# LSTM gate products in another order, sums made ahead of product 6, and VectorE work at half steps, in a four-layer graph stack

## The chip, the core and the metric

The kernel runs on one core of a Trainium2 chip. A core has TensorE (PE, matrix products into PSUM), VectorE (DVE), ScalarE (ACT, activations and copies), GpSimd (POOL) and SyncE (SP, which here issues the DMAs). They run side by side and meet at semaphores. The metric is the device time of one execution in microseconds (us), lower is better. Everything is float32.

## What is computed

`x` is 128 batches of 64 tokens with 256 channels. Four layers follow each other, each of the form `x = x + layer(relu(layernorm(x)))`: a graph convolution with batch norm, a graph network with LSTMs over windows of tokens, a causal attention, and a masked four-head attention. The change touches the second layer and the place where it begins. Its core:

```python
def _lstm_last(Wih, Whh, bih, bhh, xs):
    bias = bih + bhh
    def step(carry, x_t):
        h, c = carry
        g = x_t @ Wih.T + h @ Whh.T + bias
        i, f, gg, o = jnp.split(g, 4, axis=-1)
        c = sigmoid(f) * c + sigmoid(i) * tanh(gg)
        h = sigmoid(o) * tanh(c)
        return ((h, c), None)
    ...                                   # zero initial state, last h returned

h = relu(einsum('ts,bsh->bth', adj, x @ Wg0 + bg0))
h = relu(einsum('ts,bsh->bth', adj, h @ Wg1 + bg1))
for p in range(1, MAX_SKIP + 1):          # windows of 1, 2, 3 and 4 tokens
    nw = Tv // p
    wins = h[:, :nw * p, :].reshape(Bv * nw, p, Hd)
    last = _lstm_last(Wih[p-1], Whh[p-1], bih[p-1], bhh[p-1], wins)
    idx = jnp.arange(nw) * p + (p - 1)
    h = h.at[:, idx, :].set(last.reshape(Bv, nw, Hd))
```

Each window length overwrites tokens that the next one reads, and inside a window the tokens follow each other: a chain of recurrences. The batch is cut into 16 chunks of 8 batches. Two chunks make a super-chunk, and the LSTMs run super-chunk by super-chunk (eight of them). In a super-chunk a step multiplies 512 columns in windows of 2, 336 in windows of 3 and 256 in windows of 4.

## The kernel before

**Seven products instead of eight.** A gate's 256 x 256 weight matrix is cut into 2 x 2 blocks of 128, and the columns into two halves. The kernel uses a scheme with 7 products of blocks in place of 8 (numbered 1 to 7), which costs sums on VectorE. A `Unit` is one gate at one token step. Its products go to three PSUM banks: 5 to bank `y`; 2 and 3 to the two halves of bank `z`; 1, 6, 7 and 4 one on top of the other into bank `x`. Each bank's name exists twice. A product has an x part (the token) and an h part (the state); the first token of a window has no h part.

```python
class Unit:
    def __init__(self, q, s):
        self.q, self.s = q, s
        self.banks, self.of = {}, {1: "x", 6: "x", 7: "x", 4: "x", 5: "y", 2: "z", 3: "z"}

    def psum(self, kind):
        return self.banks[self.of[kind]][:, m:n] if kind == 3 else self.banks[self.of[kind]][:, :m]

    def product(self, kind, parts="xh"):
        ...
            nc.tensor.matmul(folded(self.psum(kind)), wsets[p, self.q][:, BLOCKS[kind][i], :],
                             (ox[self.s] if part == "x" else oh)[kind], start=first,
                             stop=(part == "h"), skip_group_check=True)          # L1155

    def copy(self, kind):                                                          # L1161, ScalarE
        nc.scalar.copy(gate(self.q, kind // 5, halves[kind // 5]), self.psum(kind))

    def add(self, dst, a, kind):                                                   # L1164, VectorE
        nc.vector.tensor_add(gate(self.q, *dst), gate(self.q, *a), self.psum(kind))

    def c11(self):
        self.add((0, halves[0]), (0, halves[0]), 2)
    def u4(self):
        self.add((0, halves[1]), (1, halves[1]), 6)
    def c12(self):
        self.add((0, halves[1]), (0, halves[1]), 3)
    def c22(self):
        self.add((1, halves[1]), (1, halves[1]), 7)

    def act(self, part):                                                           # L1084, ScalarE
        if part == 0:
            act(self.q, 0, every, gate(self.q, 0))
        elif part == 1:
            act(self.q, 1, halves[1], gate(self.q, 1, halves[1]))
        else:
            act(self.q, 1, halves[0], self.psum(4))
```

Product 6 adds onto product 1 in bank `x`, so it must come after `copy(1)`; 7 adds onto 6 and must come after the sum that reads 6; 4 must come after `c22`.

**A token step.** Pair A is the gates i and g, pair B the gates f and o. `each(us, f, ...)` applies one function after the other, each to all units of the pair. The order in the program is the order on every engine. At a `yield` other work of the kernel is put in.

```python
A = [Unit(q, 1) for q in (0, 2)]
each(A, pe(5, "x"), pe(3, "x"), pe(2, "x"))
yield
for s in range(1, p):
    last = s == p - 1
    B = [Unit(q, s) for q in (1, 3)]
    if not last:
        ox[s + 1] = operands_x(p, hv, name, s + 1)          # GpSimd
    each(A, pe(5, "h"), do("copy", 5), pe(1), do("copy", 1), pe(3, "h"), pe(6, "x"), pe(6, "h"),
         pe(2, "h"), do("u4"), do("c11"), do("c12"))
    each(B, pe(5), do("copy", 5))
    each(A, do("act", 0), pe(7), do("c22"), do("act", 1))
    each(B[:1], pe(3), pe(2))
    each(A, pe(4), do("act", 2))
    if last:
        load_sets(2)
    nc.gpsimd.tensor_mul(gates[:, 0, :, :n], gates[:, 0, :, :n], gates[:, 2, :, :n])
    each(B[1:], pe(3), pe(2))
    each(B, pe(1), do("copy", 1))
    yield
    each(B, pe(6))
    A = [] if last else [Unit(q, s + 1) for q in (0, 2)]
    each(A, pe(5, "x"))
    ...                                    # cell(): c = c * f, c = c + i * g (VectorE), tanh (ScalarE)
    if last:
        each(B[:1], do("u4"), do("c11"), pe(7))
        each(B[1:], do("u4"), pe(7))
        each(B[:1], do("c22"), do("c12"), do("act", 0))
        each(B[1:], do("c22"), do("c11"), do("c12"), do("act", 0))
        cell(0, every)
    else:
        for u in B:
            each([u], do("u4"), do("c11"), do("c12"), do("act", 0))
        cell(0, every)
        each(B, pe(7), do("c22"))
    each(B, do("act", 1))
    each(A[:1], pe(3, "x"), pe(2, "x"))
    new_state(s, 0, every)
    if not last:
        dh[0]()                            # sums of the new state for the next step, VectorE
    each(A[1:], pe(3, "x"), pe(2, "x"))
    each(B, pe(4))
    ...                                    # act(2), cell and state of the other channel half, dh[1], dh[2]
    yield
```

**What is put in.** While a super-chunk's LSTMs run, the graph convolutions of the next one, the residual sums of the one before and the layernorm of the third layer are put in at numbered yields. Numbers 0 to 3 belong to windows of 1; 4 and 5 open windows of 2, and its only step has 6 in its middle and 7 at its end; windows of 3 have 8 to 13, windows of 4 have 14 to 21. The tables give for each unit of such work its number:

```python
RESIDUAL = (0, 3, 4), (2, 5, 6)
CONV = (3, 4, 4, 5, 6, 7, 8, 9, 10, 10), (3, 4, 4, 11, 12, 13, 14, 15, 16, 17, 18, 20)
BEGUN = (11, 13, 14, 16), (17, 19)
BEGUN_FIRST = (12, 15, 16, 18), (19, 21)
FIRST = (1, 3, 3, 4, 4, 5, 6, 7, 8, 9, 10, 11, 12, 12), (3, 6, 7, 8, 10, 13, 14, 15, 16, 17, 18, 19, 20, 20)
...
START = (0, 1, 0, 0, 0, 1, 0, 1, 1, 0, 0, 1, 1, 0, 1)        # convolutions of chunks 0 and 1, ahead of the LSTMs
```

A convolution's units are, in order: batch norm scale and transposes (VectorE) and a DMA out and back; a sum; layernorm statistics; two halves of the layernorm apply (ScalarE); aggregation (TensorE); copies; product v; its bound (VectorE); product u; its bias (VectorE); a second aggregation; two activations. `FIRST` is the table of the first super-chunk.

Of the kernel before, what the change touches and what calls it, by code (L numbers as in the profile page):

```python
# [19 lines left out]
def kernel(  # L20
# [23 lines left out]
    B, T, D = x.shape  # L44
# [544 lines left out]
    with tc.manual_schedule(engines={mybir.EngineType.PE, mybir.EngineType.DVE,  # L589
# [27 lines left out]
        for c in range(2, NCH - 1):  # L617
            a, z = sevens[c], sevens.get(c - 1)
# [146 lines left out]
    with tc.manual_schedule(engines={mybir.EngineType.PE, mybir.EngineType.DVE,  # L765
# [3 lines left out]
        for c in range(2, NCH - 1):  # L769
            a, b, z = sevens[c], sevens.get(c + 1), sevens.get(c - 1)  # L770
# [121 lines left out]
    hTs = {}  # L892
# [157 lines left out]
    def lstm(p, hv, name, follows, x1, ending):  # L1050
# [3 lines left out]
        n = nb * nw  # L1054
# [85 lines left out]
        class Unit:  # L1140
# [25 lines left out]
            def c11(self):  # L1166
                self.add((0, halves[0]), (0, halves[0]), 2)

            def u4(self):
                self.add((0, halves[1]), (1, halves[1]), 6)  # L1170

            def c12(self):
                self.add((0, halves[1]), (0, halves[1]), 3)

            def c22(self):
                self.add((1, halves[1]), (1, halves[1]), 7)
# [9 lines left out]
        def each(us, *fs):  # L1186
            for f in fs:
                for u in us:
                    f(u)

        def pe(kind, parts="xh"):
            return lambda u: u.product(kind, parts)

        def do(f, *a):
            return lambda u: getattr(u, f)(*a)
# [4 lines left out]
        for s in range(1, p):  # L1200
            last = s == p - 1
            B = [Unit(q, s) for q in (1, 3)]
            if not last:
                ox[s + 1] = operands_x(p, hv, name, s + 1)
            each(A, pe(5, "h"), do("copy", 5), pe(1), do("copy", 1), pe(3, "h"), pe(6, "x"), pe(6, "h"),
                 pe(2, "h"), do("u4"), do("c11"), do("c12"))
            each(B, pe(5), do("copy", 5))
            each(A, do("act", 0), pe(7), do("c22"), do("act", 1))
            each(B[:1], pe(3), pe(2))
            each(A, pe(4), do("act", 2))  # L1210
            if last:
                load_sets(2)
            nc.gpsimd.tensor_mul(gates[:, 0, :, :n], gates[:, 0, :, :n], gates[:, 2, :, :n])  # L1213
            each(B[1:], pe(3), pe(2))
            each(B, pe(1), do("copy", 1))
            yield
            each(B, pe(6))
            A = [] if last else [Unit(q, s + 1) for q in (0, 2)]
            each(A, pe(5, "x"))

            def cell(c, part):
                nc.vector.tensor_mul(cells[:, c, part], cells[:, c, part], gate(1, c, part))
                nc.vector.tensor_add(cells[:, c, part], cells[:, c, part], gate(0, c, part))  # L1223
                nc.scalar.activation(gate(2, c, part), cells[:, c, part], AF.Tanh)  # L1224

            if last:

                each(B[:1], do("u4"), do("c11"), pe(7))
                each(B[1:], do("u4"), pe(7))
                each(B[:1], do("c22"), do("c12"), do("act", 0))  # L1230
                each(B[1:], do("c22"), do("c11"), do("c12"), do("act", 0))
                cell(0, every)
            else:
                for u in B:
                    each([u], do("u4"), do("c11"), do("c12"), do("act", 0))
                cell(0, every)
                each(B, pe(7), do("c22"))
            each(B, do("act", 1))
            each(A[:1], pe(3, "x"), pe(2, "x"))
            new_state(s, 0, every)  # L1240
            if not last:
                dh[0]()
            each(A[1:], pe(3, "x"), pe(2, "x"))
            each(B, pe(4))
            B[0].act(2)
            cell(1, halves[1])
            B[1].act(2)
            cell(1, halves[0])
            new_state(s, 1, halves[1])
            if not last:  # L1250
                dh[1]()
            new_state(s, 1, halves[0], nc.gpsimd if follows and last else nc.vector)
            if last:
                load_sets(2)
                ending()
            else:
                dh[2]()
            yield
# [212 lines left out]

    RESIDUAL = (0, 3, 4), (2, 5, 6)
    CONV = (3, 4, 4, 5, 6, 7, 8, 9, 10, 10), (3, 4, 4, 11, 12, 13, 14, 15, 16, 17, 18, 20)
    BEGUN = (11, 13, 14, 16), (17, 19)
    BEGUN_FIRST = (12, 15, 16, 18), (19, 21)
    FIRST = (1, 3, 3, 4, 4, 5, 6, 7, 8, 9, 10, 11, 12, 12), (3, 6, 7, 8, 10, 13, 14, 15, 16, 17, 18, 19, 20, 20)
    AHEAD = (4, 5, 7, 12, 14, 15), (6, 7)
    LATE = 5, 6, 8, 9  # L1480
    IDLE = {5: 4, 7: 18, 9: 10, 13: 14, 15: 8}
    FINAL = (4, 5, 10, 12, 12, 14), (6, 7, 11, 14, 14, 16)
    START = (0, 1, 0, 0, 0, 1, 0, 1, 1, 0, 0, 1, 1, 0, 1)

    tc.no_sync_barrier()
    with tc.manual_schedule(engines={mybir.EngineType.PE, mybir.EngineType.DVE, mybir.EngineType.Pool,
# [21 lines left out]
    with tc.manual_schedule(engines={mybir.EngineType.PE, mybir.EngineType.DVE, mybir.EngineType.Pool,  # L1508
                                     mybir.EngineType.Activation, mybir.EngineType.SP}):
        last = NCH // SUP - 1  # L1510
        for sc in range(last + 1):
# [23 lines left out]
            if sc + 1 < last:  # L1535
                for i in range(SUP):
                    units((BEGUN if sc else BEGUN_FIRST)[i], convs[(sc + 2) * SUP + i])
            for n, _ in enumerate(lstms(sc, hTs[sc])):
                for u in todo.pop(n, ()):
                    next(u)  # L1540
                if sc == last and n in IDLE:
                    keep_busy(IDLE[n], f"l{n}")
                if sc == last and n == 8:

                    new_hT(sc + 1)
                    for c in range(SUP):
                        load2(c, hTs[sc + 1][:, c, :].rearrange("p (q n) -> p q n", q=Q))
# [530 lines left out]
```

## Time and profile before

The median of 3 runs is 1892.07 us (1891.79 to 1892.09).

| engine | busy us | share of the span | instructions |
|---|---|---|---|
| TensorE, matmul | 1863.0 | 99% | 15077 |
| TensorE, weight load | 1479.3 | 78% | 15077 |
| VectorE | 1236.6 | 65% | 3150 |
| ScalarE | 1016.6 | 54% | 2284 |
| GpSimd | 551.4 | 29% | 704 |

The profile is one execution, with a span of 1890.8 us. The LSTM products of line 1155 run from 306 to 1516 us. In the timeline each line names the start, the duration, the engine, the source line, output and input, the shape and the count; in brackets stands how long the engine had been idle and what ended it. In the groups the columns are the count, the busy time, the mean of one in ns, the idle time before them and what ended it. A product's end is modelled, so a busy TensorE may still start late; the spacing of starts shows it.

### The profile page before, as it was taken

How to read it: one execution, taken by the hardware profiler on the slowest of the kernel's cores; microseconds unless marked ns; L12 is line 12 of the kernel's file. 1: busy time of each engine (PE TensorE's matmuls, PEld its weight loads, DVE VectorE, ACT ScalarE, POOL GpSimd, SP SyncE). 2: the span in 40 equal slices, each digit the busy share in tenths (PEclk: the TensorE clock that was granted, in tenths of full speed). 3: DMA queues.
4: the chain of work that ended last, by engine and by line, in shares of the span. 5: the costliest groups of instructions: out<-in, count | busy, mean ns of one | idle time of the engine just before them, and what ended most of it. 6: DMA issues, size and time to landing. Idle time of an engine off the chain costs nothing.

```text
span 1890.8 us, 39088 instructions
## 1 busy us (share of the span) xinstructions
PE 1863.0 (99%) x15077; PEld 1479.3 (78%) x15077; DVE 1236.6 (65%) x3150; ACT 1016.6 (54%) x2284; POOL 551.4 (29%) x704
## 2 busy tenths in 40 slices
PE   8999989999999999999999999999999999999998
PEld 6877856886897798699589689878969967777776
DVE  6768845567476666667667666665565567676776
ACT  5766544456456446555655645655565544444453
POOL 5856622122222212212322321222122114332232
PEclk9999999999999999999999999999999999999999
DMA  3224643135333433332433343343144254444433
GB/s 114 73 66 150 234 175 105 49 116 184 106 129 139 151 129 129 110 124 114 151 118 139 141 151 129 129 135 117 52 135 154 71 157 135 143 148 142 139 113 113
DMA packets 111273, 241.45 MB, mean 128 GB/s; under 512 B 11504, under 2 KB 74864, under 8 KB 111088
## 3 DMA queue, kind: packets, MB, share of 16 engines
q1 hardware_dynamic: 110192, 237.09, 37.4%
q8 instruction: 119, 1.95, 0.4%
q0 software_dynamic: 320, 1.05, 0.2%
q10 hardware_dynamic: 576, 0.82, 0.1%
q14 instruction: 66, 0.54, 0.1%
HBM read 170.50 MB, written 68.42 MB: 126 GB/s over the span
## 4 chain that ended last, share of the span: by engine, by line
PE 90%; DVE 5%; ACT 2%; issue 1%; POOL 1%; DMA 1%; SPq 0%; DVEq 0%; ACTq 0%
PE x L1155 23%; PE z L1155 11%; PE g L1126 9%; PE y L1155 6%; PE v L1568 6%; PE x L1329 4%; PE y L1329 3%; PE u L929 3%; PE p_q L1575 3%; PE v L915 3%; PE X L1764 3%; PE X L423 2%; PE X L499 2%; PE Y L1764 1%; PE Y L423 1%
## 5 line engine op out<-in xcount | busy, mean ns | idle before, releaser
L1164 DVE TENSOR_TENSOR gates<-gates,x 128x128 f32<-128x128 f32 (+2 forms) x384 | 118.5, 321 | 326.3 <-PE x L1155 319.1
L1155 PE MATMUL x<-xd,wset 128*128 128x128 f32 (+2 forms) x1152 | 256.8, 311 | 0.7 <-DVE gates L1164 0.2
L1155 PE MATMUL x<-hd,wset 128*128 128x128 f32 (+2 forms) x1152 | 246.7, 303 | 0.0
L1213 POOL TENSOR_TENSOR gates<-gates 128x512 f32<-128x512 f32 (+2 forms) x48 | 75.0, 1562 | 551.8 <-ACT gates L1084 551.8
L1084 ACT ACTIVATE gates<-gates,bias 128x256 f32<-128x256 f32 (+4 forms) x384 | 170.3, 490 | 56.2 <-DVE gates L1164 52.7
L1155 PEld LDWEIGHTS x<-xd,wset 128*128 128x128 f32 x1152 | 180.8, 190 | 19.0 <-DVE gates L1164 6.1
L1155 PEld LDWEIGHTS x<-hd,wset 128*128 128x128 f32 x1152 | 185.1, 191 | 5.0
L1126 PE MATMUL g<-hT,wset 128*128 128x256 f32 (+2 forms) x576 | 183.9, 474 | 1.1 <-DVE hT L1095 1.1
L1126 PEld LDWEIGHTS g<-hT,wset 128*128 128x128 f32 x576 | 108.6, 190 | 69.8 <-issue 38.5
L1161 ACT COPY gates<-y 128x128 f32<-128x128 f32 (+2 forms) x192 | 54.3, 294 | 202.3 <-PE y L1155 201.8
L1155 PE MATMUL z<-hs,wset 128*128 128x128 f32 (+2 forms) x768 | 154.0, 303 | 0.0
L1155 PE MATMUL z<-hT,wset 128*128 128x128 f32 (+2 forms) x768 | 148.4, 306 | 0.0
L1155 PEld LDWEIGHTS z<-hs,wset 128*128 128x128 f32 x768 | 119.8, 191 | 3.3
L1155 PEld LDWEIGHTS z<-hT,wset 128*128 128x128 f32 x768 | 117.9, 192 | 4.4 <-ACT gates L1113 0.5
L1161 ACT COPY gates<-x 128x128 f32<-128x128 f32 (+2 forms) x192 | 56.6, 296 | 93.5 <-PE x L1155 92.8
L1164 DVE TENSOR_TENSOR gates<-gates,z 128x128 f32<-128x128 f32 (+2 forms) x384 | 104.5, 316 | 0.1
L1084 ACT ACTIVATE gates<-x,bias 128x128 f32<-128x128 f32 (+2 forms) x192 | 74.8, 390 | 49.3 <-PE x L1155 46.5
L1113 ACT ACTIVATE gates<-g,bias 128x512 f32<-128x512 f32 (+2 forms) x144 | 74.6, 560 | 30.7 <-PE g L1126 30.2
L1155 PE MATMUL x<-hT,wset 128*128 128x128 f32 (+2 forms) x384 | 85.7, 305 | 0.4 <-ACT gates L1084 0.2
L1155 PE MATMUL x<-hs,wset 128*128 128x128 f32 (+2 forms) x384 | 84.9, 303 | 0.0
L1224 ACT ACTIVATE gates<-cell 128x256 f32<-128x256 f32 (+2 forms) x144 | 55.3, 384 | 51.9 <-DVE cell L1223 50.3
L1155 PE MATMUL y<-xd,wset 128*128 128x128 f32 (+2 forms) x384 | 77.4, 304 | 3.9 <-ACT gates L1113 3.3
(326 smaller groups left out, 4144.6 us busy)
## 6 DMA issues: line engine op xcount, KB each, us to landing
wset<-wfar SPq DMA_DIRECT2D x96, 960.0 KB, 6.5
hT<-far_h SPq DMA_DIRECT2D x124, 128.0 KB, 3.1
far_h<-hm SPq DMA_DIRECT2D x16, 512.0 KB, 2.8
far_n<-xs SPq DMA_DIRECT2D x16, 512.0 KB, 3.5
xs<-far_n SPq DMA_DIRECT2D x64, 128.0 KB, 3.7
far_x<-xs SPq DMA_DIRECT2D x16, 512.0 KB, 3.0
x<-far_x SPq DMA_DIRECT2D x64, 128.0 KB, 3.2
xt<-in_x_dram SPq DMA_DIRECT2D x15, 512.0 KB, 4.1
```

Source lines behind the costliest of these rows:

```text
L423: nc.tensor.matmul(self.banks[tag][:, i * CH // 2 : (i + 1) * CH // 2], w, self.at[kind], start=first and not i, stop=True, skip_group_che ...
L915: nc.tensor.matmul(banks[m], wg0_sb[:, k, m * P : (m + 1) * P], agg[:, k, :], start=(k == 0), stop=(k == KD - 1))
L1084: nc.scalar.activation(gate(q, c, part), src, AF.Tanh if q == 2 else AF.Sigmoid, bias=bs[:, q * KD + c : q * KD + c + 1])
L1113: nc.scalar.activation(columns_of(gate(q, c)), natural(banks[q, c][:, :n].rearrange("p (w b) -> p w b", b=nb)), AF.Tanh if q == 2 else AF. ...
L1126: nc.tensor.matmul(banks[q, c][:, :n].rearrange("p (w b) -> p w b", b=nb), wsets[p, q][:, 2 * k + c, :], hv[:, k, : (nw - 1) * p + 1 : p, ...
L1155: nc.tensor.matmul(folded(self.psum(kind)), wsets[p, self.q][:, BLOCKS[kind][i], :], (ox[self.s] if part == "x" else oh)[kind], start=firs ...
L1161: nc.scalar.copy(gate(self.q, kind // 5, halves[kind // 5]), self.psum(kind))
L1164: nc.vector.tensor_add(gate(self.q, *dst), gate(self.q, *a), self.psum(kind))
L1213: nc.gpsimd.tensor_mul(gates[:, 0, :, :n], gates[:, 0, :, :n], gates[:, 2, :, :n])
L1329: nc.tensor.matmul(folded(ps(g, kind)), wih1[:, g, KINDS1[kind], :], right[kind], start=kind in (2, 5, 1), stop=True, skip_group_check=True)
L1568: nc.tensor.matmul(ps[:, i, :], hT[:, k, j, :], w[:, k, first : first + D], start=(k == 0), stop=(k == KD - 1))
L1764: nc.tensor.matmul(st[c, tag][:, i * CH // 2 : (i + 1) * CH // 2].rearrange("p (a n) -> p a n", n=P), w, st[c, "o7"][kind], start=first an ...
```

## The change

The sums of a gate are taken in another order. With `v5` the sum of blocks 5 and 3 is made first, and `u5` adds product 6 to it, where before `u4` added 6 to 5 and `c12` added 3 after it. So the sums with 2, 3 and 5 can be made before product 6 is there, and after it one sum is left instead of three. The products 3 and 2, which share bank `z`, both come before the first sum that reads the bank. Between the products 1 and 6 of pair B the second unit's product 3 now stands (and its product 2, except in the last step of a window, where product 2 stands between 6 and 7).

A new `yield "a"` in the first half of a step gets half numbers (5.5, 9.5, 11.5 and so on); VectorE work that stood in the second half of a step moves there. In the first super-chunk, the first unit of the convolution of chunk 2 moves into the start phase, and the chunk's other units one place ahead.

```diff
-            def u4(self):
-                self.add((0, halves[1]), (1, halves[1]), 6)
-
-            def c12(self):
-                self.add((0, halves[1]), (0, halves[1]), 3)
+            def v5(self):
+                self.add((0, halves[1]), (1, halves[1]), 3)
+
+            def u5(self):
+                self.add((0, halves[1]), (0, halves[1]), 6)
...
-            each(A, pe(5, "h"), do("copy", 5), pe(1), do("copy", 1), pe(3, "h"), pe(6, "x"), pe(6, "h"),
-                 pe(2, "h"), do("u4"), do("c11"), do("c12"))
+            each(A, pe(5, "h"), do("copy", 5), pe(1), do("copy", 1), pe(3, "h"), pe(2, "h"), do("v5"),
+                 do("c11"), pe(6), do("u5"))
             each(B, pe(5), do("copy", 5))
             each(A, do("act", 0), pe(7), do("c22"), do("act", 1))
-            each(B[:1], pe(3), pe(2))
+            yield "a"
+            each(B[:1], pe(3))
             each(A, pe(4), do("act", 2))
             if last:
                 load_sets(2)
             nc.gpsimd.tensor_mul(gates[:, 0, :, :n], gates[:, 0, :, :n], gates[:, 2, :, :n])
-            each(B[1:], pe(3), pe(2))
+            each(B[:1], pe(2), do("v5"))
             each(B, pe(1), do("copy", 1))
+            each(B[:1], do("c11"))
+            each(B[1:], pe(3))
+            if not last:
+                each(B[1:], pe(2), do("v5"), do("c11"))
             yield
             each(B, pe(6))
+            if last:
+                each(B[1:], pe(2))
             A = [] if last else [Unit(q, s + 1) for q in (0, 2)]
             each(A, pe(5, "x"))
...
+            each(B[:1], do("u5"))
             if last:
-
-                each(B[:1], do("u4"), do("c11"), pe(7))
-                each(B[1:], do("u4"), pe(7))
-                each(B[:1], do("c22"), do("c12"), do("act", 0))
-                each(B[1:], do("c22"), do("c11"), do("c12"), do("act", 0))
+                each(B[1:], do("v5"), do("c11"))
+            each(B[1:], do("u5"))
+            each(B, do("act", 0), pe(7))
+            if last:
+                each(B, do("c22"))
                 cell(0, every)
             else:
-                for u in B:
-                    each([u], do("u4"), do("c11"), do("c12"), do("act", 0))
                 cell(0, every)
-                each(B, pe(7), do("c22"))
+                each(B, do("c22"))
...
-    RESIDUAL = (0, 3, 4), (2, 5, 6)
-    CONV = (3, 4, 4, 5, 6, 7, 8, 9, 10, 10), (3, 4, 4, 11, 12, 13, 14, 15, 16, 17, 18, 20)
+    RESIDUAL = (0, 3, 4), (2, 5, 5.5)
+    CONV = (3, 4, 4, 5, 5.5, 7, 8, 9, 10, 10), (3, 4, 4, 11, 11.5, 13, 14, 15, 15.5, 17, 18, 20)
     BEGUN = (11, 13, 14, 16), (17, 19)
-    BEGUN_FIRST = (12, 15, 16, 18), (19, 21)
-    FIRST = (1, 3, 3, 4, 4, 5, 6, 7, 8, 9, 10, 11, 12, 12), (3, 6, 7, 8, 10, 13, 14, 15, 16, 17, 18, 19, 20, 20)
+    BEGUN_FIRST = (11.5, 15, 17, 18), (19, 21)
+    FIRST = (1, 2, 3, 4, 5, 5.5, 7, 8, 9, 9.5, 11, 12, 12), (3, 5.5, 7, 8, 10, 13, 14, 15, 15.5, 17, 17.5, 19, 20, 20)
...
-    START = (0, 1, 0, 0, 0, 1, 0, 1, 1, 0, 0, 1, 1, 0, 1)
+    START = (0, 1, 0, 0, 0, 1, 0, 1, 1, 0, 0, 1, 1, 0, 1, 2)
...
-            for n, _ in enumerate(lstms(sc, hTs[sc])):
+            n = -1
+            for mark in lstms(sc, hTs[sc]):
+                n = n + 0.5 if mark else int(n) + 1
```

## The prediction

> **What bounds the kernel now.** I read the page's busy shares first, then its chain, then the costliest groups.
>
> ```profile
> PE 1863.0 (99%) x15077; PEld 1479.3 (78%) x15077; DVE 1236.6 (65%) x3150; ACT 1016.6 (54%) x2284; POOL 551.4 (29%) x704
> ...
> PE 90%; DVE 5%; ACT 2%; issue 1%; POOL 1%; DMA 1%; SPq 0%; DVEq 0%; ACTq 0%
> ...
> L1164 DVE TENSOR_TENSOR gates<-gates,x 128x128 f32<-128x128 f32 (+2 forms) x384 | 118.5, 321 | 326.3 <-PE x L1155 319.1
> ```
>
> TensorE is the bound and no product is removed, so only TensorE's own gaps can be won. VectorE idles 319.1 us waiting for the products of L1155, which by itself costs nothing. "99%" hides gaps, because each record's modelled end reaches past the next start. So I went to the timeline and measured starts. A product (x part and h part) is four records; back to back they start every 0.112 us at 128 columns (window 4), 0.143 at 168 (window 3), 0.216 at 256 (window 2). An ordinary step of window 4:
>
> ```profile
> 872.28 0.39 PE L1155 MATMUL x<-hT,wset 128*128 128x128 f32 x2
> ...
> 872.48 0.27 ACT L1161 COPY gates<-x 128x128 f32<-128x128 f32 x1 [0.97 <-PE x L1155]
> 872.50 0.39 PE L1155 MATMUL x<-hs,wset 128*128 128x128 f32 x2
> ...
> 872.80 0.49 PE L1155 MATMUL x<-xd,wset 128*128 128x128 f32 x2
> ...
> 875.75 0.48 DVE L1164 TENSOR_TENSOR gates<-gates,x 128x128 f32<-128x128 f32 x2
> ...
> 876.08 0.49 PE L1155 MATMUL x<-xd,wset 128*128 128x128 f32 x2
> ```
>
> At 872.80 product 6 of pair B starts 0.30 after 872.50, not 0.22, because it waits for the copy that ends at 872.75; the pair then takes 0.49, not 0.39: the record after a late one is another 0.10 late. So a wait costs its lateness plus 0.10. Product 4 at 876.08 does the same after the sum c22. The last step of a window has a third such place, product 7 at 901.68:
>
> ```profile
> 901.34 0.29 DVE L1164 TENSOR_TENSOR gates<-gates,x 128x128 f32<-128x128 f32 x1 [3.97 <-PE x L1155]
> ...
> 901.68 0.49 PE L1155 MATMUL x<-xd,wset 128*128 128x128 f32 x2
> ...
> 902.77 0.49 PE L1155 MATMUL x<-xd,wset 128*128 128x128 f32 x2
> ```
>
> Summing spacing beyond the regular pace over all 5376 records of L1155 gives 34.0 us, about 3.5 in each of the eight super-chunks and 8.0 in the first. That is 1.8% of 1892, and the ceiling of the main part of the change. By place, over the run: ordinary steps, product 6 of B 3.5 and product 4 of B 4.0; last steps of windows 3 and 4, product 6 of B 2.1, 7 of B 3.7, 4 of B 2.4; product 7 of pair A in step 2 of window 4, 1.6; start of its step 3, 3.3; product 5 right after an aggregation, 4.8 (not touched); the rest is small, but for the first super-chunk:
>
> ```profile
> 306.19 2.39 ACT L1113 ACTIVATE gates<-g,bias 128x512 f32<-128x512 f32 x4
> ...
> 307.00 1.18 PE L1155 MATMUL y<-xd,wset 128*128 128x256 f32 x4 [2.51 <-ACT gates L1113]
> ...
> 308.06 3.59 PE L1155 MATMUL z<-hT,wset 128*128 128x256 f32 x8
> ```
>
> ```profile
> 308.30:311.70 3.40, 3.40 (x12) 2.13 (x15) 2.69 (x5) 2.58 (x5) 0.00 (x0) 0.50 0.99 230
> ```
>
> ScalarE stood behind four layernorm applies (304.21 to 306.28) of convolution chunk 2, TensorE idled 2.5 us, and then ran at a granted clock of 0.50 (the third number from the end) for 3.4 us: eight z records each 0.21 late, 1.7 us. Together about 4.5 us.
>
> **What the Trainium skill says.** "Perfetto Trace Analysis", Identifying the Most-Contended Engine: matmul busy time is no measure of nearness to the roof. The trace agrees: 99% busy, with 34 us of late starts in one line. "TensorE: Matmul & The Clock Gate", Part 2, LDWEIGHTS: TensorE pulls the next weight load ahead of running matmuls. The 0.10 us after each late record fits a load that could not be pulled ahead; that reading is mine. The same page, Part 1: an idle window of about 3.4 us drops the clock to half. Here it was 0.50 for 3.4 us after only 2.5 us of idling; the measured state decides. "PSUM — Partial Sum Buffer", bank collisions: accesses of two engines must be guarded by bank, not by address. That explains the order "both products of a bank, then its reads". Whether the program really waits by bank no view of this kernel shows, as it never reads one half of bank z between the products 3 and 2. I take it as likely and use it below.
>
> **The change, part by part.** Counts of matmuls, copies, sums and activations do not change; only orders do. Latencies from the timeline at 128 columns: start of a product's last record to the VectorE sum 0.38, to a ScalarE copy 0.31; sum 0.29, or 0.20 apart in a row; copy 0.27; end to the waiting product 0.05.
>
> *Ordinary steps (window 3 step 1, window 4 steps 1 and 2).* Products 3 and 2 of B's second unit now lie between products 1 and 6, so copy 1 has 0.89 us more: it ends long before product 6. After product 6 VectorE has two sums left instead of six. With product 6 of B at 0: u5 of the two units at 0.72 and 1.16, sigmoid 1.04 to 1.55, cell product 1.59, cell sum 2.12, c22 2.46 to 2.74, so product 4 may start at 2.80, where TensorE arrives at 3.13. Both waits vanish: -3.5 - 4.0 = -7.5 us.
>
> *Last steps (one per window).* Product 2 of B's second unit fills the place between 6 and 7. That removes the waits at 6, 7 (first unit) and 4, 8.2 us, plus 0.3 in window 2. But product 7 of the second unit must wait for u5 of that unit, which VectorE takes only after v5 and c11, and these need product 2. Window 4, product 6 at 0: the last record of product 2 starts at 1.23, v5 at 1.61, c11 1.81, u5 2.01 to 2.29, product 7 at 2.34 against 1.79: late by 0.55 + 0.10 = 0.65. By the same count in windows 3 and 2 also about 0.65. Three per super-chunk: 3 x 0.65 x 8 = +15.6. If v5 is not held by product 2, one sum less: 0.47, 0.41 and 0.29, +9.3. Net +7 or +1.
>
> *Pair A, start of a step.* u5 now comes fifth of six sums, not first, and must be done before product 7 of A. With VectorE free there is 0.6 us of slack. Where other VectorE work comes first there is less:
>
> ```profile
> 882.30 0.45 DVE L1164 TENSOR_TENSOR gates<-gates,x 128x128 f32<-128x128 f32 x2
> ...
> 882.60 0.30 PEld L1155 LDWEIGHTS x<-xd,wset 128*128 128x128 f32 x2 [0.25 <-DVE gates L1164]
> ```
>
> Here (window 4 step 2) a scaling and two transposes end at 882.3. Four sums more ahead would make it 0.8 worse in the five super-chunks where it occurs, +4. Against this stands that the whole recurrence (c22, cell, tanh, state) ends about 1.4 us earlier by my count above, and so this work starts earlier. I take -1. The start of step 3 (3.3 us) waits for the same recurrence: I take -1.5.
>
> *Other VectorE work moved to the half steps.* Taken out of the second half it no longer stands behind v5 and c11 in VectorE's queue. In the old kernel it already ran at that time (its sums L935 began at 869.56, right after c22 of A): no gain of its own, a condition of the first part.
>
> *First super-chunk.* The first unit of convolution chunk 2 moves into the start phase, where VectorE is idle between 274.1 and 279.6 and the unit needs 2.3 (286.54 to 288.88). Its chain then runs one place earlier throughout, the applies come before ScalarE is needed, and the wait with its half clock goes: -4.5. The late first product 5 at 291.38 (0.46), held by sums behind the same unit, goes too: -0.5.
>
> Sum with the bank rule: -7.5 + 7 - 1 - 1.5 - 5 = -8. Without it: -14. I weigh them about 2 to 1: -10, so 1882.
>
> **Rivals.** (1) The new wait at product 7 eats the gain: the change only moves waits in the last steps. For it: VectorE's queue order; against it: one product earlier everything else. With VectorE slower than counted (L1223 and L1222 take 0.43 and 0.55 beside GpSimd at 877.3 and 877.7) and no gain at the clock: about 1890. (2) Pair A becomes the bound: 0.5 to 1 us more at product 7 of A in several steps, 8 to 15 us: 1890 to 1897. For it: the 882.6 wait; against it: in the other steps the slack is 0.5 us or more. (3) All waits named go and no new one counts: -7.5 - 8 - 1.6 - 3.3 - 5 = -25, 1867. Against it: u5 of the second unit can't precede its product 2.
>
> **Range and chances.** The three rivals span 1867 to 1897. Each needs several places to err the same way, so 1873 to 1891 should hold 8 in 10. To be faster by 2% it would have to save 38 us, more than all 34 us of late starts; slower by 2% would need about 0.8 us of new waiting in each of the 48 token steps.
>
> **What will show it.** A super-chunk lasts 155.57 us now (start of window 2 to the next, in the middle of the run): I expect 0.4 to 1.2 less. No 0.49 pairs at products 6 and 4 of B in ordinary steps; a new one at the second product 7 of each last step, waiting on L1164 for 0.3 to 0.6; no clock of 0.50 near 308. I am wrong if pair A's product 7 waits in most steps, if VectorE's queue delays the state at a step's end, or if the first super-chunk finds another wait.

## The result: 0.4% slower, and where the time went

The changed kernel takes 1899.49 us (median of 4 runs, 1899.12 to 1900.02), beside 1891.93 us for the kernel before. The ratio is 1.0042 with a 95% interval of 1.0024 to 1.0059: 7.6 us more, where 10 us less was predicted. It lies above the predicted range of 1873 to 1891.

From the page of the changed kernel: the busy times, the chain that ended last, and three groups (the products of `x`, and the sums that read `z` and `x`; the last columns are the idle time before them and what ended most of it).

```profile
PE 1857.2 (98%) x15077; PEld 1478.1 (78%) x15077; DVE 1253.9 (66%) x3150; ACT 1020.8 (54%) x2284; POOL 548.0 (29%) x704
...
PE 87%; DVE 7%; ACT 2%; issue 1%; POOL 1%; DMA 1%; SPq 0%; DVEq 0%; ACTq 0%
...
L1155 PE MATMUL x<-xd,wset 128*128 128x128 f32 (+2 forms) x1152 | 260.8, 308 | 17.1 <-DVE gates L1164 16.6
L1164 DVE TENSOR_TENSOR gates<-gates,z 128x128 f32<-128x128 f32 (+2 forms) x384 | 108.1, 319 | 188.6 <-PE z L1155 141.3
...
L1164 DVE TENSOR_TENSOR gates<-gates,x 128x128 f32<-128x128 f32 (+2 forms) x384 | 117.0, 321 | 116.4 <-PE x L1155 115.4
```

Counts of instructions are the same. TensorE is still the bound, but the chain's VectorE share went from 5% to 7%, and the products of bank `x` now show 16.6 us of idling behind the sums of L1164; before there were 0.2 us. VectorE's own idling before the sums that read `x` fell from 326.3 to 116.4 us, but most of it only moved to the sums that read `z` and now come first: 188.6 us, where the kernel before had 0.1. TensorE's waits, added up (waiting line, what ended it, us in all, times, the longest):

```profile
PE x L1155 <- DVE gates L1164: 16.6, 40, 1.3
PE g L1126 <- DMA wset<-wfar: 3.1, 1, 3.1
```

The second line is one wait for weights, in the first super-chunk, which the kernel before did not have. This view sees only a part, since a record that starts late often counts as no idling. Measured as in the prediction, as spacing of the starts beyond the regular pace, the late starts of L1155 rose from 34.0 to 40.5 us; an ordinary super-chunk has 5.0 where it had 3.5, and lasts 157.05 us where it lasted 155.56. By place, in us over the whole run:

| place | before | after |
|---|---|---|
| product 6 of B (ordinary and last steps) | 5.6 | 0 |
| first product 7 of B, last steps | 3.7 | 0 |
| second product 7 of B, last steps | 0.3 | 14.2 |
| product 4 of B, ordinary steps | 4.0 | 3.0 |
| product 4 of B, last steps | 2.4 | 2.45 |
| product 7 of A (window 4 steps 2 and 3, window 3 step 2) | 1.6 | 9.1 |
| product 7 of B in the last super-chunk, ordinary steps | 0 | 2.6 |
| start of step 3 of window 4 (products 1 and 5 of A) | 3.3 | 1.15 |
| first super-chunk: weights (L1126), with the half clock after them | 0 | 4.9 |

An ordinary step of the changed kernel, window 4 step 1, in the timeline:

```profile
719.39 0.39 PE L1155 MATMUL x<-xd,wset 128*128 128x128 f32 x2
...
719.59 0.49 DVE L1164 TENSOR_TENSOR gates<-gates,z 128x128 f32<-128x128 f32 x2 [0.76 <-PE z L1155]
...
719.99 0.16 DVE L194 SCALAR_TENSOR_TENSOR nmr_b<-mv_b,rstd_b 128x4 f32<-128x4 f32 x1
...
720.06 0.70 DVE L1164 TENSOR_TENSOR gates<-gates,x 128x128 f32<-128x128 f32 x2
720.18 1.09 ACT L196 ACTIVATE cv<-xs,nmr_b,rstd_b 128x256 f32<-128x256 f32 x2 [1.22 <-DVE nmr_b L194]
...
721.18 0.89 ACT L1084 ACTIVATE gates<-gates,bias 128x256 f32<-128x256 f32 x2
...
722.57 0.48 DVE L1164 TENSOR_TENSOR gates<-gates,x 128x128 f32<-128x128 f32 x2
...
722.91 0.49 PE L1155 MATMUL x<-xd,wset 128*128 128x128 f32 x2 [0.24 <-DVE gates L1164]
```

Product 6 of B at 719.39 starts on time and its pair takes 0.39, so the copy no longer holds it: that half of the plan worked. Then a small operation that belongs to the work put in, the shift `nmr` of a layernorm (0.16 us), stands in VectorE's queue behind v5 and c11 and just ahead of the two sums with product 6. ScalarE has idled 1.22 us for it; then it makes two layernorm applies (1.09 us from 720.18), and the sigmoids of pair B stand in its queue behind them (721.18). So they begin 1.79 us after product 6, where the prediction counted 1.04, and the kernel before had 1.54. Product 4 at 722.91 is late and takes 0.49, as before. Pair A of the next step:

```profile
729.12 0.84 DVE L1164 TENSOR_TENSOR gates<-gates,z 128x128 f32<-128x128 f32 x4
...
729.89 0.47 DVE L1164 TENSOR_TENSOR gates<-gates,x 128x128 f32<-128x128 f32 x2
...
730.22 0.49 PE L1155 MATMUL x<-xd,wset 128*128 128x128 f32 x2 [0.84 <-DVE gates L1164]
```

The two sums that product 7 of A needs (reading `x`, at 729.89) stand behind four sums that read `z`, which take 0.84 us, and TensorE idles 0.84 us for them. Beyond the regular pace, with the record after it, that is 1.11 us each time, in five super-chunks; the kernel before lost 0.32 here. And the last step of a window:

```profile
748.92 0.49 DVE L1164 TENSOR_TENSOR gates<-gates,z 128x128 f32<-128x128 f32 x2 [0.60 <-PE z L1155]
...
749.32 0.48 DVE L1164 TENSOR_TENSOR gates<-gates,x 128x128 f32<-128x128 f32 x2
...
749.65 0.49 PE L1155 MATMUL x<-xd,wset 128*128 128x128 f32 x2 [0.33 <-DVE gates L1164]
...
750.75 0.49 PE L1155 MATMUL x<-xd,wset 128*128 128x128 f32 x2
```

VectorE had been idle 0.60 us for product 2 of the second unit; then v5, c11 and u5 follow in a row and product 7 starts late at 749.65. The first super-chunk, first where the old wait stood and then where a new one came:

```profile
303.93 1.03 PE L1155 MATMUL y<-xd,wset 128*128 128x256 f32 x4
304.80 1.89 PE L1155 MATMUL z<-hT,wset 128*128 128x256 f32 x8
...
377.22 2.14 SPq L887 DMA_DIRECT2D wset<-wfar  x4
...
379.47 1.99 PE L1126 MATMUL g<-hT,wset 128*128 128x256 f32 x8 [0.16 <-DVE hT L1095]
...
384.56 3.79 PE L1126 MATMUL g<-hT,wset 128*128 128x256 f32 x11 [3.09 <-DMA wset<-wfar]
```

The eight `z` records take 1.89 us at the full clock, not 3.59. But the weights of window 4, issued at 377.22, hold TensorE up at 384.56. In SyncE's queue they now stand behind a store (372.17), four loads (from 374.90) and one more load (376.69) of a later convolution, whose first unit the change moved from number 12 to 11.5 (`BEGUN_FIRST`); in the kernel before the first two of these four weight issues came at 376.43, ahead of that store at 377.41. After 3.1 us of idling the clock fell again (windows view: the window and its length, busy time and count of PE, PEld, DVE, ACT and POOL, clock, DMA share, GB/s):

```profile
386.00:389.40 3.40, 3.40 (x10) 2.74 (x9) 0.51 (x2) 2.02 (x5) 0.00 (x0) 0.52 0.99 413
```

So the first super-chunk took 162.88 us (159.69 before), after it had begun its windows of 2 earlier by 3.07 us.

### The profile page after: what moved, and what is told of

Same layout as the page of the kernel before. It is cut to its first block, busy times and chain, and to the rows that moved or that the text cites. A ratio compares the mean times of both kernels' runs of the same rounds, so it can differ in the third digit from the quotient of the medians.

```text
span 1897.5 us, 39094 instructions
## 1 busy us (share of the span) xinstructions
PE 1857.2 (98%) x15077; PEld 1478.1 (78%) x15077; DVE 1253.9 (66%) x3150; ACT 1020.8 (54%) x2284; POOL 548.0 (29%) x704
## 4 chain that ended last, share of the span: by engine, by line
PE 87%; DVE 7%; ACT 2%; issue 1%; POOL 1%; DMA 1%; SPq 0%; DVEq 0%; ACTq 0%
PE x L1155 21%; PE z L1155 11%; PE g L1126 9%; PE y L1155 5%; PE v L1576 5%; PE x L1335 4%; PE y L1335 3%; PE v L915 3%; PE u L929 3%; PE p_q L1583 3%; PE X L1772 3%; PE X L423 2%; PE X L499 2%; DVE gates L1164 2%; PE Y L1772 1%
## 5 line engine op out<-in xcount | busy, mean ns | idle before, releaser
L1155 PE MATMUL x<-xd,wset 128*128 128x128 f32 (+2 forms) x1152 | 260.8, 308 | 17.1 <-DVE gates L1164 16.6
L1155 PE MATMUL x<-hd,wset 128*128 128x128 f32 (+2 forms) x1152 | 254.7, 303 | 0.0
L1164 DVE TENSOR_TENSOR gates<-gates,z 128x128 f32<-128x128 f32 (+2 forms) x384 | 108.1, 319 | 188.6 <-PE z L1155 141.3
L1155 PEld LDWEIGHTS x<-xd,wset 128*128 128x128 f32 x1152 | 186.3, 191 | 34.3 <-DVE gates L1164 27.8
L1164 DVE TENSOR_TENSOR gates<-gates,x 128x128 f32<-128x128 f32 (+2 forms) x384 | 117.0, 321 | 116.4 <-PE x L1155 115.4
L1155 PEld LDWEIGHTS x<-hd,wset 128*128 128x128 f32 x1152 | 187.8, 191 | 5.0
L1126 PE MATMUL g<-hT,wset 128*128 128x256 f32 (+2 forms) x576 | 185.6, 477 | 3.3 <-DMA wset<-wfar 3.1
L1126 PEld LDWEIGHTS g<-hT,wset 128*128 128x128 f32 x576 | 109.8, 192 | 72.2 <-issue 42.1
L1155 PE MATMUL z<-hT,wset 128*128 128x128 f32 (+2 forms) x768 | 146.7, 303 | 0.0
L1155 PE MATMUL z<-hs,wset 128*128 128x128 f32 (+2 forms) x768 | 146.5, 303 | 0.2 <-DVE hs L1093 0.2
L1155 PEld LDWEIGHTS z<-hT,wset 128*128 128x128 f32 x768 | 117.2, 191 | 3.7
L1155 PEld LDWEIGHTS z<-hs,wset 128*128 128x128 f32 x768 | 117.2, 191 | 3.6 <-DVE hs L1093 0.3
L1155 PE MATMUL x<-hT,wset 128*128 128x128 f32 (+2 forms) x384 | 85.7, 305 | 0.2 <-ACT gates L1084 0.2
L1155 PE MATMUL x<-hs,wset 128*128 128x128 f32 (+2 forms) x384 | 84.9, 303 | 0.0
L1155 PE MATMUL y<-hd,wset 128*128 128x128 f32 (+2 forms) x384 | 79.4, 309 | 0.0
```

Source lines behind the costliest of these rows:

```text
L1126: nc.tensor.matmul(banks[q, c][:, :n].rearrange("p (w b) -> p w b", b=nb), wsets[p, q][:, 2 * k + c, :], hv[:, k, : (nw - 1) * p + 1 : p, ...
```

## The experiments

The theory after the comparison was that five separate waits, each caused by an order in a queue, make up the loss and hide a gain: pair A's sums, product 7 of the last steps, the shift ahead of product 6's sums, the DMA issues of the first super-chunk, and units of the last super-chunk that stayed at whole numbers. The general rival was that the waits only shift the recurrence: take one away and the next holds the same chain, so that little comes back. Each is undone alone, then all together; some runs try a second way or ask about one part. All ratios are to the kernel before, so the changed kernel stands at 1.0042. Its interval reaches from 1.0024 to 1.0059, so for the savings of 3 to 5 us below the waits that go in the traces weigh more than the times.

**Pair A's sums in the old order.** Only the order of pair A's sums goes back; its products keep the new order (2 ahead of 6), and everything else stays as changed.

```diff
-            each(A, ..., pe(3, "h"), pe(2, "h"), do("v5"), do("c11"), pe(6), do("u5"))
+            each(A, ..., pe(3, "h"), pe(2, "h"), pe(6), do("u4"), do("c11"), do("c12"))
```

> The changed kernel (1899.5 us) with one part undone: pair A takes its sums in the old order (block 5 plus product 6 first, then 2, then 3). Theory: in pair A, u5 stands fifth behind four sums, and where other VectorE work comes first this makes product 7 of A late; the trace of the changed kernel shows 5.6 us at step 2 and 2.8 us at step 3 of windows of 4, 0.7 at step 2 of windows of 3. Then the waits fall to about 1.6 us in all and the time to about 1892. Rival: the recurrence itself ends late and VectorE is busy anyway, the order within pair A does not matter: 1898 to 1900.

Measured: 1891.43 us, ratio 0.9999 (0.9991 to 1.0008), 0.43% or 8.1 us below the changed kernel. TensorE's idling behind the sums of L1164 falls from 16.6 to 11.3 us. Product 7 of A in window 4 step 2 is back at 1.6 us, the ones in step 3 and in window 3 are gone, and the late starts of L1155 fall from 40.5 to 33.1. So no new wait took its place. The rest of the saving (8.1 against 7.4) lies behind the LSTMs, in a stretch that is 1.0 us shorter in this run; the part on the sum below comes back to it. This one line of the program undoes the whole loss.

**The second unit of the last step summed in the old way.** u4 (5 + 6) directly after product 6, then product 7, and the sums with 2 and 3 behind it.

```diff
             if last:
-                each(B[1:], do("v5"), do("c11"))
-            each(B[1:], do("u5"))
-            each(B, do("act", 0), pe(7))
+                each(B[1:], do("u4"))
+                each(B[:1], do("act", 0))
+                each(B, pe(7))
+                each(B[1:], do("c11"), do("c12"), do("act", 0))
```

(`c22` follows, and ordinary steps keep the changed order.)

> The changed kernel with another order of VectorE in the last step of a window, second unit of pair B: block 5 plus product 6 first, then product 7 may go, and the sums with 2 and 3 after it. TensorE's order is as in the changed kernel. Theory: the second product 7 waits for a sum that stands behind two sums that need product 2; the trace shows 14.2 us of this (0.59 in each of 24 last steps). It goes, against up to 2.5 us that may come back at product 4: about 1886 to 1888. Rival: the wait only moves to the sums after it and to the state at the end of the step, so that less than 4 us are won: 1896 or more.

Measured: 1884.89 us, ratio 0.9962 (0.9949 to 0.9975), 0.80% or some 15 us below the changed kernel. Its last step:

```profile
744.84 0.29 DVE L1164 TENSOR_TENSOR gates<-gates,x 128x128 f32<-128x128 f32 x1 [0.75 <-PE x L1155]
...
745.35 0.29 DVE L1164 TENSOR_TENSOR gates<-gates,x 128x128 f32<-128x128 f32 x1 [0.23 <-PE x L1155]
...
745.53 0.39 PE L1155 MATMUL x<-xd,wset 128*128 128x128 f32 x2
...
745.73 0.48 DVE L1164 TENSOR_TENSOR gates<-gates,z 128x128 f32<-128x128 f32 x2
...
745.98 0.39 PE L1155 MATMUL x<-xd,wset 128*128 128x128 f32 x2
```

Each sum with product 6 now waits only for its product (the `x` sums at 744.84 and 745.35), the sums that read `z` come behind, and both products 7 run in pairs of 0.39. The late starts fall by 14.4 us, to 26.1, and a super-chunk takes 155.29 us. Product 4 keeps its wait of 2.57 us, and it doesn't grow by what product 7 no longer waits.

**Product 2 of the last step as early as in ordinary steps.** Another way to the same end: product 2 of the second unit, v5 and c11 ahead of product 6.

```diff
             each(B[1:], pe(3))
-            if not last:
-                each(B[1:], pe(2), do("v5"), do("c11"))
+            each(B[1:], pe(2), do("v5"), do("c11"))
             yield
             each(B, pe(6))
-            if last:
-                each(B[1:], pe(2))
...
-            if last:
-                each(B[1:], do("v5"), do("c11"))
```

> The changed kernel with TensorE's order in the last step of a window as in ordinary steps: product 2 of pair B's second unit before product 6, with v5 and c11 there. Theory: the wait at the second product 7 comes only from product 2 standing between 6 and 7; it goes (14.2 us), and in its place the first product 7 has nothing between it and product 6, and waits for u5 by 0.27 in windows of 4 and 0.17 in windows of 3 (3.5 us in all): about 1889. Rival: VectorE is the bound of the last step, and the wait stays wherever product 2 stands: 1896 or more.

Measured: 1889.34 us, ratio 0.9986 (0.9978 to 0.9993), 0.56% or 10.6 us less. The wait at the second product 7 is gone. At the first product 7 one of 2.45 us in all appears, since nothing stands any more between the products 6 and 7 of the pair; I had expected 3.5. The run before it, with the old sums there, is 4.5 us better; it keeps product 2 as a filler and lets no sum that is due wait for it. These waits explain about 2.5 of the 4.5.

**Is it the bank or the data?** v5 reads the half of bank `z` that product 3 wrote, not that of product 2. In the changed kernel product 2 stands ahead of v5 in the program. Here only that order is turned; v5 stays as it is.

```diff
             if last:
-                each(B[1:], pe(2))
+                each(B[1:], do("v5"), pe(2))
...
             if last:
-                each(B[1:], do("v5"), do("c11"))
+                each(B[1:], do("c11"))
```

> The changed kernel, but in the last step v5 of pair B's second unit stands in the program ahead of product 2 of that unit, which shares its bank. Theory: a read of a bank waits for every product that stands ahead of it in the program and writes this bank, also to the other half; v5 then no longer waits for product 2, one sum fewer lies between product 2 and the second product 7, and the wait there falls from 0.59 to about 0.4, 0.4 and 0.3 in windows of 4, 3 and 2: 4 to 5 us less, about 1895. Rival: waits go by the half that is read, v5 was already early: 1899 to 1900.

Measured: 1894.02 us, ratio 1.0014 (1.0006 to 1.0023), 0.28% or 5.3 us less. The wait at the second product 7 falls from 14.2 to 9.7 us: 0.47, 0.43 and 0.32 each in windows of 4, 3 and 2. Its last step:

```profile
746.34 0.29 DVE L1164 TENSOR_TENSOR gates<-gates,z 128x128 f32<-128x128 f32 x1 [0.67 <-PE z L1155]
...
746.54 0.48 DVE L1164 TENSOR_TENSOR gates<-gates,x 128x128 f32<-128x128 f32 x2
...
746.88 0.49 PE L1155 MATMUL x<-xd,wset 128*128 128x128 f32 x2 [0.20 <-DVE gates L1164]
```

Only one sum (c11) now waits for product 2, where two did. The prediction's count without the bank rule was 9.3 us for this place; so in the changed kernel the read of one half did wait for the product that the program put ahead of it in the other half. The rest of the wait is plain order: c11, which nobody needs soon, stands in the queue ahead of u5, and it needs product 2.

**The shift of the layernorm on GpSimd.** To take the small operation out of VectorE's queue.

```diff
-        nc.vector.scalar_tensor_tensor(nmr, mv[:, :, 0], -1.0, rstd, op0=OP.mult, op1=OP.mult)
+        nc.gpsimd.tensor_tensor(nmr, mv[:, :, 0], rstd, OP.mult)      # right behind the statistics
+        nc.gpsimd.tensor_scalar(nmr, nmr, -1.0, None, op0=OP.mult)
```

> The changed kernel, but the small layernorm shift (128x4) in front of the applies of convolutions and of the third layer is made by GpSimd right after the statistics, not by VectorE at the place of the applies. Theory: at number 16 the shift stands in VectorE's queue behind v5 and c11, the applies of ScalarE start late, the sigmoids of pair B behind them too, and so product 4 of B (2.5 us at step 1 of windows of 4); with the shift made earlier these go, and the recurrence ends earlier, so that product 7 of A in step 2 wins 1 to 2 us as well: about 1895. Rival: ScalarE is late for another reason: no change, 1899 to 1900.

Measured: 1898.67 us, ratio 1.0033 (1.0021 to 1.0045), 0.09% less, inside the uncertainty: a miss in the total. Product 4 of B in window 4 step 1 lost its wait (2.51 to 0), so that cause was right. But about 3 us of new waits came at the start of the windows of 2, at products 5 and 3: 0.78 in each of four super-chunks. One of them:

```profile
777.55 2.08 ACT L201 ACTIVATE cv<-xs,nmr_b,rstd_b 128x256 f32<-128x256 f32 x4 [5.38 <-POOL nmr_b L194]
```

The applies wait for GpSimd's two operations, which take 0.76 and 0.55 us there (from 776.13), beside a sum on VectorE; behind the applies stand the activations that product 5 waits for. In two other super-chunks, where that VectorE sum begins about when they end, the two operations take 0.20 and 0.24 us, and product 5 is on time. So the new cost is a later shift again, in front of ScalarE. The next run makes the shift early without GpSimd.

**The shift on VectorE, but at the half step.** The shift becomes a unit of its own, with a number in the first half of the step (the tables get one number more for it).

```diff
         nc.vector.scalar_tensor_tensor(nmr, mv[:, :, 0], -1.0, rstd, op0=OP.mult, op1=OP.mult)
+        yield
...
-    BEGUN = (11, 13, 14, 16), (17, 19)
+    BEGUN = (11, 13, 14, 15.5, 16), (17, 19)
```

(`BEGUN_FIRST` 17.5, `AHEAD` and the first of `FINAL` 11.5, `LATE` 5.5; elsewhere at a whole number.)

> The changed kernel with the small layernorm shift still on VectorE, but as a unit of its own at the half step ahead of the applies (15.5 for 16, 11.5 for 12, 5.5 for 6). With the shift on GpSimd the wait at product 4 of step 1 of windows of 4 went, but one of 2.8 us came up at the start of windows of 2. Theory: behind v5 and c11 in VectorE's queue the shift holds up ScalarE's applies and with them the sigmoids; made at the half step it costs nothing elsewhere: product 4 there loses its 2.5 us and the start of windows of 2 stays free; 1896 to 1897. Rival: what was won at product 4 is lost at the next wait of the recurrence anyway: 1899 or more.

Measured: 1895.54 us, ratio 1.0022 (1.0015 to 1.0029), 0.20% or 3.8 us less. Window 4 step 1 (lines stand one number later here):

```profile
717.95 0.39 PE L1156 MATMUL x<-xd,wset 128*128 128x128 f32 x2
...
718.92 0.95 ACT L1085 ACTIVATE gates<-gates,bias 128x256 f32<-128x256 f32 x2 [0.35 <-DVE gates L1165]
```

The applies now begin at 717.48, ahead of product 6, and the sigmoids 0.97 us after it, where the changed kernel had 1.79. The waits at product 4 of B in steps 1 and 2 of window 4 (six places) are gone and none comes at the start of the windows of 2; the late starts fall to 36.6. An operation of 0.16 us had cost these 3.8, because 1.09 us of ScalarE work waited for it with the sigmoids behind.

**The DMA issues of the first super-chunk.** The store and the loads go back behind the first two of the four weight issues, which then come at 370.51, not 377.22.

```diff
-    BEGUN_FIRST = (11.5, 15, 17, 18), (19, 21)
+    BEGUN_FIRST = (12, 15, 17, 18), (19, 21)
```

> The changed kernel with one number put back: in the first super-chunk the first unit of the next convolution at 12, not 11.5. Theory: at 11.5 its transfers enter the DMA issue queue ahead of two weight sets, the weight sets for windows of 4 land late, TensorE idles 3.1 us and then runs at half clock for 3.4 us: about 4.9 us go, 1894.6. Rival: the weights are late because other transfers fill the DMA engines at that time, whatever the order of issue: 1899 to 1900.

Measured: 1894.73 us, ratio 1.0016 (1.0009 to 1.0022), 0.26% or 4.9 us less. The same products of L1126, which fell into two stretches with 3.09 us of waiting between them, now run through:

```profile
379.70 5.45 PE L1126 MATMUL g<-hT,wset 128*128 128x256 f32 x24 [0.16 <-DVE hT L1095]
```

The first super-chunk takes 158.27 us where the changed kernel took 162.88.

**The part in the start phase alone, on the kernel before.** Only the first unit of chunk 2 moves into the start phase and its chain one place ahead; no sums and no half steps are changed.

```diff
-    FIRST = (1, 3, 3, 4, 4, 5, 6, 7, 8, 9, 10, 11, 12, 12), (...)
+    FIRST = (1, 2, 3, 4, 5, 6, 7, 8, 9, 10, 11, 12, 12), (...)
-    START = (0, 1, 0, 0, 0, 1, 0, 1, 1, 0, 0, 1, 1, 0, 1)
+    START = (0, 1, 0, 0, 0, 1, 0, 1, 1, 0, 0, 1, 1, 0, 1, 2)
```

> The kernel before (1891.5 us) with one part of the change alone: the first unit of convolution chunk 2 in the start phase, and that chunk's other units one place ahead, at whole numbers. Theory: the wait at the start of windows of 2 in the first super-chunk and the half clock after it go, with one small wait before it: about 1886.5. Rival: the unit only delays the start phase by its 2.3 us of VectorE, and half is lost again: 1889 or more.

Measured: 1887.11 us, ratio 0.9976 (0.9966 to 0.9985): 4.5 us faster than the kernel before. The late starts of the first super-chunk fall from 7.98 to 3.67, which is all of it. So this part of the change is a gain of its own and needs none of the others.

**The last super-chunk.** Two units of the third layer's layernorm (statistics and transposes), which had stayed behind the middle of a step, move to the half step.

```diff
-    FINAL = (4, 5, 10, 12, 12, 14), (6, 7, 11, 14, 14, 16)
+    FINAL = (4, 5, 9.5, 12, 12, 14), (6, 7, 11, 14, 14, 15.5)
```

> The changed kernel with two units of the last super-chunk at half numbers, 10 at 9.5 (statistics) and 16 at 15.5 (transposes). Theory: VectorE work left in the second half of a step now stands behind v5 and c11 and ahead of u5, and product 7 of B waits for u5 (1.6 and 1.0 us in the last super-chunk): about 2.5 us less, 1897. Rival: the end of the last super-chunk is set by the transfers that these units start, or the later work takes the time back: 1899 or more.

Measured: 1896.52 us, ratio 1.0026 (1.0017 to 1.0036), 0.16% or 3.0 us less. The waits at product 7 of B there (1.57 and 1.01 us) are gone, and the late starts of the last super-chunk fall from 8.12 to 5.36.

**All of them together.** Pair A and the last step in the old order of sums, the half step for the shift and for the last super-chunk, the DMA issues back; from the change remain the order of pair B's ordinary steps and of the first unit in its last steps, the order of pair A's products, the half steps and the start phase.

> The changed kernel with its new waits undone together: pair A in the old order of sums; in the last step block 5 plus product 6 first; the first unit of the next convolution in the first super-chunk at 12; the small layernorm shift as a unit of its own at the half step ahead of the applies; and in the last super-chunk the statistics at 9.5 and the transposes at 15.5. Theory: the savings measured one by one add up, 8 + 14.5 + 4.8, with about 3 for product 4 of B and 2.6 for product 7 of B in the last super-chunk: 1866 to 1869. Rival: the waits overlap and uncover each other, so that a third or more is lost: 1876 or more.

Measured: 1866.29 us (1865.9 to 1866.72), ratio 0.9866 (0.9851 to 0.9881): 1.3% faster than the kernel before, and 1.8% below the changed one. From its page (the span is 1864.7 us):

```profile
L1156 PE MATMUL x<-xd,wset 128*128 128x128 f32 (+2 forms) x1152 | 256.8, 305 | 0.6 <-DVE gates L1165 0.6
```

(Lines stand one number later here; L1156 is L1155 of the others.) The idling behind the sums went from 16.6 to 0.6 us, the late starts from 40.5 to 13.5, and a super-chunk takes 153.49 us. The single savings, 8.1 + 15 + 4.9 + 3.8 + 3.0 = 34.8 us, would have given 1864.7; measured are 33.2 of them. They add up within the uncertainty, which the rival of a wait that only moves on could not give.

## Why the prediction was wrong, point by point

- **Ordinary steps, -7.5: about -4.5, and 2.6 against it.** The wait at product 6 of B vanished in full (3.5). That at product 4 fell only from 4.0 to 3.0. The step that failed is "a condition of the first part": all VectorE work put in was taken as out of the second half, yet the shift stayed there, and in the last super-chunk whole units stayed. Both are shown by their runs (3.8 and 3.0 us). The count after product 6 followed VectorE's queue alone and left out ScalarE's: the applies that wait for the shift stand ahead of B's sigmoids, which begin 1.79 us after product 6 instead of 1.04. With nothing in between they begin after 0.97 and product 4 is on time, so the count itself was good.
- **Last steps, net +7: about +8.** This step was right. The new wait at the second product 7 was put at 0.65 us and measured 0.59 each, 14.2 in all against 15.6. The choice of the bank rule at 2 to 1 was right too: the order of v5 and product 2 alone made 14.2 into 9.7. The Trainium skill ("PSUM — Partial Sum Buffer", bank collisions) asks for PSUM to be guarded by bank and not by address; the program's wait agrees with that, with 4.5 us as its price here. Only product 4 was expected to lose its wait and kept it (2.45).
- **Pair A, -1: +7.5.** The step that failed the most. The prediction had the number, "0.8 worse in the five super-chunks", which gives +4: measured are 1.11 us each where 0.32 stood, 5.56 - 1.61 = +3.95 us in step 2. It then took this back with "the whole recurrence ... ends about 1.4 us earlier". That isn't so. In window 4 step 1, in the five super-chunks with this wait, the last sum of the state ends 1.86 us after the h part of the next product 5 of A starts, before and after alike; in step 2 the number goes from 2.33 to 2.10. The end of that chain hangs on product 4 and what follows it, and TensorE takes product 4 in its own order. With the shift at the half step c22 is done 0.27 us before TensorE gets to product 4, and the state still ends 1.75 us after product 5 starts; the wait at product 7 of A falls only from 1.11 to 1.00. What became earlier lies ahead of product 4 and ends in waiting for it. The slack of "0.5 us or more" in other steps was also too hopeful: step 3 of window 4 (2.80) and step 2 of window 3 (0.73) had none. One line of the program (the first run) takes the lateness at these places from 9.1 back to 1.6 us, and 8.1 us in all.
- **Start of step 3, -1.5: -2.2.** Right, a little small.
- **First super-chunk, -5: -5.1, and +4.9 against it.** The gain was there: the windows of 2 begin 3.07 us earlier and their step takes 36.29 in place of 38.31 us; alone on the kernel before it brought 4.5. Not seen was that `BEGUN_FIRST` at 11.5 also moves DMA issues in SyncE's queue ahead of weights that are due, 4.9 us by its run. The prediction counted VectorE work at the moved numbers, and a unit carries its DMAs along.
- **The sum.** With +7.5 for -1 (8.5 more), +4.9 for the weights, 3.0 + 2.6 for the two misses of ordinary steps, 1 more in the last steps and 0.8 less in the two last terms, -8 becomes some +11. By the starts of its records the changed kernel is 9.5 us behind at the last step of the last window of 4 (the 1.7 us between aren't placed), and 6.7 at the end: about 2.8 us come back after the LSTMs. There, in the attention, TensorE's waits that the profile puts down to `issue`, at the products of the scores, are 2.3 us in two places before and 0.9 in one after; with pair A's sums in the old order they are gone, and the stretch behind the LSTMs is another 1.0 us shorter. No run tested that; its cause is open.
- **The rivals.** The second ("pair A becomes the bound", 1890 to 1897) named the largest error and was given too little weight, and the first (the new wait at product 7) came true beside it. The range took the errors as independent; they all err the same way, since each new order puts something ahead in a queue. "Each needs several places to err the same way" was the reason for the narrow range, and it is what happened.

## What to carry to other kernels

Where an engine that works in program order feeds a bound one, the sum that the next product waits for must stand first in the queue. Making other sums "ahead" of it is worth it only where the engine is through with them before that product is done. Where their operands come late (the last steps) or the engine is still busy with other work (pair A), the needed sum waits for them. When work is moved to another place, list everything that the unit carries, its smallest operation and its DMA issues too, and look what it then stands in front of, on every engine: 0.16 us on VectorE held up ScalarE's queue. A count that "the chain ends earlier" has to be followed to the last instruction of the chain that the next step waits for, not to the first that gets faster.

## What was not expected of the hardware

The granted clock fell to half again (0.52, for 3.4 us) after 3.1 us of idling, as it had after 2.5 in the kernel before; it makes a wait of 3.1 us cost 4.9. And an operation of 0.16 us on VectorE took, as two on GpSimd, 0.20 and 0.24 us where the VectorE sum next to them came later, and 0.76 and 0.55 us where they ran beside it; that took away the wait that it was meant for, and brought about 3 us of others elsewhere.
